# How the last sums of a mixture of experts are split between TensorE and VectorE, and how their rows are loaded and stored

## The chip, the cores and the metric

The kernel runs on one core of one Trainium2 chip. The metric is device time in microseconds, as the median of several runs. Beside these runs there is one profiled execution, from which the profile and the trace come. All times in views of the trace are microseconds from the start of its span.

## What is computed

The reference is a model of two layers, in fp32, on 8 sequences of 256 tokens with 256 features. Each layer is an attention-like block and a mixture of experts, and after each of the four blocks the result is added to the input and layer-normalised:

```python
x = L0_attn_x
x = _layernorm(x + _L0_attn_ref(x, ...), axis=-1)
x = _layernorm(x + _L0_ffn_ref(x, ...), axis=-1)
x = _layernorm(x + _L1_attn_ref(x, ...), axis=-1)
x = _layernorm(x + _L1_ffn_ref(x, ...), axis=-1)
```

Only the end of the last line matters here. `_L1_ffn_ref` routes every token to 4 of 16 experts, and adds a shared expert that sees all tokens:

```python
cw = _combine_weights(xt, gate_w)          # 4 nonzero weights per token
for e in range(E):
    a = _swiglu(xt @ expert_up_w[e].T)
    out = out + cw[:, e:e + 1] * (a @ expert_down_w[e].T)
out = out + _swiglu(xt @ shared_up_w.T) @ shared_down_w.T
```

So for each token four weighted rows of 256 numbers, the row of the shared expert and the token's own row are added, and the sum is normalised.

## The kernel before

The 2048 tokens are 16 tiles of 128 tokens (128 partitions), in 4 groups of 4 tiles (`GT = 4`, `NG = 4`). A group's residual rows stay in SBUF as `xg[g]`, 128 x 4 x 256. Attention, the first mixture, the state-space block and the second mixture follow each other.

In a mixture, tokens are first scattered to buckets by expert in HBM. Then tiles of 128 bucket rows run through the expert's three products; the weighted result of each row is scattered to HBM, to the tensor `m1ys`, where the four rows of a token lie side by side. The weights of all 16 experts lie meanwhile in one large SBUF tile, `big`.

What comes after the last expert tile is the tail, and the function `after1` writes it. For each of the 16 token tiles it has to:

- load the tile's results, 128 tokens x 4 rows x 256, 512 KB, from `m1ys` into a tile `m1gy` (`results`, L694, issued on SyncE's queue);
- add the four rows (`summed`): VectorE adds rows 0 and 1 to rows 2 and 3 (L751, a 128x512 add in place, "the halving add"), then TensorE multiplies each of the two halves with the identity matrix and adds them in PSUM (L756);
- add the PSUM sum to the residual row on VectorE (L759);
- normalise it (`normed`): statistics on VectorE (L720, L722), the inverse root on GpSimd (L731, L732, L734), a small product on VectorE (L733), scale and shift on ScalarE (L735);
- store the 128 KB of the finished tile from SyncE's queue (L1549).

The shared expert of the last group (tiles 12 to 15) is computed in the tail as well, with `Experts.shared`. It works on two halves of the group and three blocks of features: gate and up products (L543), a SiLU on ScalarE (L552) and a gate product on VectorE (L553), for each of six steps; and for each of the four tiles the down product (L563), into the PSUM bank to which L756 then adds the expert rows. The three steps of the first half come first; the others are interleaved with the sums of the other tiles by a list that is written out by hand, `order`: 0, 1, 12, 2, 3, 13, 4, 5, 6, 7, 14, 8, 9, 15, 10, 11. PSUM sums take turns in three banks.

Two pools of four buffers each hold the loaded results (`rowpool`, `lastrows`). Seven loads are issued ahead; each further load is issued after the code of one more tile, so on SyncE's queue loads and stores alternate:

```python
for n, i in enumerate(order):
    if i >= last:
        ...
        next(steps)
    else:
        finish(i)
    load(n + AHEAD)
```

The framework puts the instructions in order by its own priorities, engine by engine, and adds the waits. Each engine works through its list in that order. Each transfer of SyncE and ScalarE is given one of eight completion counters, in the order in which the framework places them, and waits until the transfer that had this counter before has landed.

Of the kernel before, what the change touches and what calls it, by code (L numbers as in the profile page):

```python
# [12 lines left out]
F32 = mybir.dt.float32  # L13
# [6 lines left out]
P = 128  # L20
DM = 256
KC = DM // P
NB, SEQ = 8, 256
GT = 4
# [9 lines left out]
E1, F1, TOP1, SH1 = 16, 176, 4, 352  # L34
# [53 lines left out]
M1 = Moe("m1", E1, F1, TOP1, 2, SH1, 5)  # L88
# [10 lines left out]
def kernel(  # L99
# [16 lines left out]
    nc = tc.nc  # L116
# [12 lines left out]
    def bank(tag, name):  # L129
        return psum.tile([P, 512], F32, name=name, tag=tag, bufs=BANKS[tag])  # L130

    x_rows = x_in.rearrange("b s d -> (b s) d")
    out_rows = out.rearrange("b s d -> (b s) d")
# [5 lines left out]
    xg = []  # L139
# [48 lines left out]
    for m in (M0, M1):  # L188
        d = disp[m.name] = {}
        new = lambda shape, name, dt=F32: const.tile(  # L190
            shape, dt, name=f"{m.name}{name}", tag=f"{m.name}{name}"
# [86 lines left out]
    def after_all(ins, first, done):  # L278

        if first is None:  # L280
            for w in done:
                tc.add_manual_dep(ins.ins, w.ins.name, SYNC, reason="reads what was written")
            return ins
        tc.add_manual_dep(ins.ins, first.ins.name, NOSYNC, reason="behind the first")
        return first
# [401 lines left out]
            with tc.If(count > m.usual - m.sure):  # L687
                run(m.usual, m.tiles)

    def results(m, g, t, pool=None):  # L690

        d, i = disp[m.name], g * GT + t
        gy = (pool or rowpool).tile([P, m.top, DM], F32, name=f"{m.name}gy{g}_{t}", tag="r")
        ins = nc.sync.dma_start(  # L694
            gy,
            d["ys"][i * P * m.top : (i + 1) * P * m.top, :].rearrange(
                "(p k) d -> p k d", k=m.top
            ),
        )
        d["first"] = after_all(ins, d["first"], d["results"])  # L700
        return gy
# [14 lines left out]
    def normed(g, t, by_steps=False):  # L716

        x = xg[g][:, t, :]
        st = small.tile([P, 6], F32, name="st", tag="st")
        nc.vector.bn_stats(st, x)  # L720
        mv = small.tile([P, 2], F32, name="mv", tag="mv")
        nc.vector.bn_aggr(mv, st)  # L722
        rstd = small.tile([P, 1], F32, name="rstd", tag="rstd")
        off = small.tile([P, 1], F32, name="off", tag="lnoff")
        if by_steps:
            var = small.tile([P, 1], F32, name="var", tag="rstd")
            nc.vector.tensor_scalar_add(var, mv[:, 1:2], LN_EPS)
            root_by_steps(rstd, var)
            nc.vector.scalar_tensor_tensor(off, mv[:, 0:1], -1.0, rstd, ALU.mult, ALU.mult)
        else:  # L730
            nc.gpsimd.tensor_scalar_add(rstd, mv[:, 1:2], LN_EPS)  # L731
            nc.gpsimd.tensor_tensor(rstd, rstd, root[:, :1], ALU.pow)  # L732
            nc.vector.tensor_scalar_mul(off, mv[:, 0:1], -1.0)  # L733
            nc.gpsimd.tensor_tensor(off, off, rstd, ALU.mult)  # L734
        nc.scalar.activation(x, x, AF.Identity, bias=off, scale=rstd)  # L735
# [8 lines left out]
            nc.vector.tensor_add(x, x, gy[:, k, :])  # L744
        normed(g, t)

    def summed(m, g, t, gy, y=None):

        half = m.top // 2
        x = xg[g][:, t, :]  # L750
        nc.vector.tensor_add(gy[:, :half, :], gy[:, :half, :], gy[:, half:, :])  # L751
        fresh = y is None
        if fresh:
            y = bank("a", f"{m.name}sum{g}_{t}")[:, :DM]
        for k in range(half):
            nc.tensor.matmul(  # L756
                y, lhsT=ident, rhs=gy[:, k, :], start=(fresh and k == 0), stop=(k == half - 1)
            )
        nc.vector.tensor_add(x, x, y)  # L759
        normed(g, t)  # L760
# [90 lines left out]
    rowpool = ctx.enter_context(tc.tile_pool(name="rows", bufs=4))  # L851
# [6 lines left out]
    big = bigpool.tile([P, SLOTS * SLOT], F32, name="big", tag="big")  # L858
# [246 lines left out]
    def after0(ex):  # L1105
        mixer_weights()
        for t in range(3):
            first[t] = results(M0, 0, t)
# [20 lines left out]
    with ExitStack() as st:  # L1129
# [14 lines left out]
        order, free = [], {}  # L1144
# [358 lines left out]
        def all_combined(g):  # L1503
            for t in range(GT):
                for i in (t, t + 1):
                    if i < GT and (g, i) not in waits:
                        waits[g, i] = results(M0, g, i)
                yield
                (summed if g < 2 else combined)(M0, g, t, waits.pop((g, t)))
                yield  # L1510
            ready.add(("combined", g))
# [17 lines left out]
    lastrows = ctx.enter_context(tc.tile_pool(name="lastrows", bufs=4, reuse_waits="tile"))  # L1529
# [4 lines left out]
    def after1(ex):  # L1534

        last = (NG - 1) * GT
        order = [0, 1, last, 2, 3, last + 1, 4, 5, 6, 7, last + 2, 8, 9, last + 3, 10, 11]
        pools = (rowpool, lastrows)
        AHEAD = 7
        rows = {}  # L1540

        def load(n):
            if n < len(order):
                rows[order[n]] = results(M1, *divmod(order[n], GT), pools[n % 2])

        def finish(i, y=None):
            g, t = divmod(i, GT)
            summed(M1, g, t, rows.pop(i), y)
            nc.sync.dma_start(out_rows[i * P : (i + 1) * P, :], xg[g][:, t, :])  # L1549

        for n in range(AHEAD):
            load(n)
        steps = ex.shared(NG - 1, wsh1, lambda t, y: finish(last + t, y))
        for _ in range(len(M1.shblocks)):
            next(steps)
        for n, i in enumerate(order):
            if i >= last:
                if i == last + 2:
                    next(steps)
                next(steps)  # L1560
            else:
                finish(i)
            load(n + AHEAD)

    mixture(M1, wsh1, (1, 2), (), after1)


# [91 lines left out]
```

## Time and profile before

| | us |
|---|---|
| median of 3 runs | 1518.86 (1517.16 to 1519.47) |
| the profiled execution | 1588.88 |
| its span | 1587.2 |
| the tail in it: from the first TensorE work after the last expert tile | 1542.66 to 1587.2 |
| last TensorE instruction of the tail ends | 1581.10 |
| last instruction of the normalisation (ScalarE) ends | 1584.22 |

| engine | busy in the span | instructions |
|---|---|---|
| TensorE | 1440.3 us (91%) | 6482 |
| VectorE | 814.7 us (51%) | 2962 |
| ScalarE | 576.9 us (36%) | 1498 |
| GpSimd | 426.5 us (27%) | 600 |

The profile comes from one execution with the hardware profiler on, which took 70 us longer than the median run. "PE" is TensorE's products, "PEld" its weight loads, "DVE" VectorE, "ACT" ScalarE, "POOL" GpSimd, "SPq" the issue of transfers on SyncE. L751 is line 751 of the kernel. The chain of waits follows the work that ended last back from the last instruction, at each step to what released it. A row of the timeline has its start, its length, the engine, the line, the operation with output and inputs, and in brackets how long the engine had been idle before it and what ended that. The mean granted clock of TensorE in the span is 0.955 of full speed. In the tail there are 16 loads of 512 KB and 16 stores of 128 KB.

### The profile page before, as it was taken

Reading aid. Unit: us, or ns where it says so; the run is one execution under the profiler, and the core shown is the slowest. Engines: PE = TensorE matmul, PEld = TensorE weight load, DVE = VectorE, ACT = ScalarE, POOL = GpSimd, SP = SyncE. Lnnn points to the kernel's source line nnn. Section 1 sums busy time; section 2 is a strip of 40 time slices with the busy share of each in tenths; the row PEclk is TensorE's granted clock in tenths of the full one; section 3 lists DMA queues with packets and bytes.
Section 4 is the critical chain, followed back from the end, with each engine's and each line's share of the span. In section 5 each row is a group of like instructions: output and inputs, shape, how many; then the busy total and the mean of one; then the engine's idle time right before and its main releaser. Section 6 shows DMA issues by size and latency. Waiting matters only on the chain. (4 is left out here: it accounts for less than half of the span.)

```text
span 1587.2 us, 21590 instructions
## 1 busy us (share of the span) xinstructions
PE 1440.3 (91%) x6482; PEld 1020.1 (64%) x6482; DVE 814.7 (51%) x2962; ACT 576.9 (36%) x1498; POOL 426.5 (27%) x600
## 2 busy tenths in 40 slices
PE   8999999999999999997898885898979768999997
PEld 5666665666566666675677773555656557677765
DVE  3444564455544554454354544676666454444436
ACT  3333433334233423351243432556646222233322
POOL 1000005000410031104635554021151442333334
PEclk9999999999999999997999998899989789999999
DMA  9999999800100020162444445310010631233327
GB/s 362 413 413 413 413 409 391 263 1 1 58 24 1 1 90 21 71 210 74 129 142 147 140 146 183 105 66 1 1 54 3 256 124 44 79 106 96 96 81 258
DMA packets 79973, 233.50 MB, mean 147 GB/s; under 512 B 11323, under 2 KB 44378, under 8 KB 78448
## 3 DMA queue, kind: packets, MB, share of 16 engines
q1 hardware_dynamic: 63088, 189.89, 33.7%
q0 software_dynamic: 16768, 42.19, 7.4%
q8 instruction: 56, 0.92, 0.3%
q14 instruction: 61, 0.50, 0.1%
HBM read 80.29 MB, written 155.40 MB: 149 GB/s over the span
## 5 line engine op out<-in xcount | busy, mean ns | idle before, releaser
L933 PE MATMUL qkp<-xT,big 128*128 128x512 f32 x512 | 243.0, 597 | 2.1 <-issue 2.1
L968 ACT ACTIVATE pr<-neg,least 128x128 f32<-128x128 f32 (+1 forms) x256 | 114.4, 449 | 281.8 <-DVE least L963 271.1
L671 POOL DMA_INDIRECT m0ys<-m0ys,m0xl x114 | 112.5, 987 | 99.6 <-ACT m0ys L670 37.3
L933 PEld LDWEIGHTS qkp<-xT,big 128*128 128x128 f32 x512 | 91.1, 191 | 72.5 <-issue 70.4
L941 DVE COPY qk<-qkp 128x512 f32<-128x512 f32 x64 | 44.1, 690 | 178.6 <-PE qkp L933 165.5
L371 POOL DMA_INDIRECT m0xs<-m0xe,m0rows x96 | 92.8, 966 | 154.6 <-DVE pT L984 109.4
L917 PE MATMUL vp<-big,xT 128*128 128x512 f32 x256 | 118.0, 599 | 4.3 <-DVE x L1004 4.3
L999 PE MATMUL op<-big,z 128*128 128x256 f32 x512 | 120.5, 382 | 0.0
L963 DVE CUSTOM_DVE_ANT_0 neg<-sc,cmask 128x128 f32<-128x128 f32 (+1 forms) x256 | 81.3, 354 | 63.9 <-PE sc L953 60.9
L671 POOL DMA_INDIRECT m1ys<-m1ys,m1xl x74 | 72.8, 984 | 115.5 <-ACT m1ys L670 104.3
L999 PEld LDWEIGHTS op<-big,z 128*128 128x128 f32 x512 | 92.6, 190 | 14.9 <-ACT z L1021 4.8
L259 POOL TENSOR_TENSOR rstd<-rstd,numbers 128x1 f32<-128x1 f32 x16 | 8.7, 551 | 305.9 <-DVE rstd L258 305.9
L986 PE MATMUL zp<-pT,big 128*128 128x256 f32 x256 | 77.9, 386 | 2.6 <-issue 2.0
L917 PEld LDWEIGHTS vp<-big,xT 128*128 128x128 f32 x256 | 47.1, 192 | 49.2 <-issue 42.2
L953 PE MATMUL sc<-qk,qk 128*128 128x256 f32 x256 | 77.9, 387 | 0.0
L974 DVE TENSOR_SCALAR pr<-pr,total 128x128 f32<-128x128 f32 (+1 forms) x256 | 70.2, 319 | 3.4
L984 DVE COPY pT<-pt 128x384 f32<-128x384 f32 x128 | 66.9, 549 | 5.9 <-issue 2.2
L986 PEld LDWEIGHTS zp<-pT,big 128*128 128x128 f32 x256 | 48.1, 192 | 33.8 <-issue 14.1
L980 PEld LDWEIGHTS pt<-ident,pr 128*128 128x128 f32 x384 | 47.6, 142 | 33.0 <-issue 30.4
L371 POOL DMA_INDIRECT m1xs<-m1xe,m1rows x64 | 62.1, 970 | 18.7 <-issue 17.0
L949 PEld LDWEIGHTS sc<-qk,qk 128*128 128x128 f32 x256 | 44.2, 193 | 29.6 <-issue 21.1
L980 PE MATMUL pt<-ident,pr 128*128 128x128 f32 x384 | 58.1, 274 | 0.0
(2808 smaller groups left out, 3032.7 us busy)
## 6 DMA issues: line engine op xcount, KB each, us to landing
m0xs<-blank SPq DMA_DIRECT2D x9, 7740.0 KB
m1xs<-blank SPq DMA_DIRECT2D x4, 7740.0 KB
m0xl<-m0xs SPq DMA_DIRECT2D x114, 129.0 KB
m0gy<-m0ys SPq DMA_DIRECT2D x16, 768.0 KB
m1xl<-m1xs SPq DMA_DIRECT2D x74, 129.0 KB
m1gy<-m1ys SPq DMA_DIRECT2D x16, 512.0 KB
big<-in_w_moe SPq DMA_DIRECT2D x1, 5472.0 KB
big<-in_w_heads SPq DMA_DIRECT2D x12, 384.0 KB
```

The costliest lines, as they stand in the source:

```text
L371: ins = nc.gpsimd.indirect_dma_start(out=d["xs"], out_offset=bass.IndirectOffsetOnAxis(ap=rows[:, k, t : t + 1], axis=0), in_=xe[:, k, :], ...
L671: ins = nc.gpsimd.indirect_dma_start(out=d["ys"], out_offset=bass.IndirectOffsetOnAxis(ap=row[:, DM : DM + 1].bitcast(I32), axis=0), in_=y ...
L917: nc.tensor.matmul(ps, lhsT=xT[:, k, t * P : (t + 1) * P], rhs=w_vq[q][:, k, :], start=(k == 0), stop=(k == KC - 1),)
L933: nc.tensor.matmul(ps, lhsT=w_qk[h][:, at : at + P], rhs=xT[:, k, :], start=(k == 0), stop=(k == KC - 1),)
L953: nc.tensor.matmul(sc[:, P:], lhsT=qT[:, c0 + P : c0 + SEQ], rhs=kT[:, c0 : c0 + SEQ], start=True, stop=True,)
L963: nc.vector.tensor_tensor_reduce(out=neg[:, cols], in0=sc[:, cols], in1=cmask[:, cols], scale=-SCALE, scalar=3.0e38, op0=ALU.add, op1=ALU.min,
L968: nc.scalar.activation(pr[:, cols], neg[:, cols], AF.Exp, bias=least[:, i : i + 1], scale=-1.0, accum_out=total[:, i : i + 1],)
L974: nc.vector.tensor_scalar_mul(pr[:, cols], pr[:, cols], total[:, i : i + 1])
L980: nc.tensor.transpose(pt[:, i * P : (i + 1) * P], pr[:, i * P : (i + 1) * P], ident)
L984: pace[0] = nc.vector.tensor_copy(pT, pt)
L986: nc.tensor.matmul(zps[:, b * SEQ : (b + 1) * SEQ], lhsT=vs[2 * b][:, cols], rhs=pT[:, : 2 * P], start=True, stop=False,)
L999: nc.tensor.matmul(ps[:, :DM], lhsT=zs[i][:, t * P : (t + 1) * P], rhs=w_o[q * QH + i], start=(i == 0), stop=(i == QH - 1),)
```

## The change

Four things change, all in the tail:

- For tiles with an odd number the halving add is left out, and TensorE adds all four rows with four products instead of two. Tiles with an even number are summed as before.
- The loaded results no longer take turns in two pools. Each of the 16 tiles has its own place in `big`, whose expert weights are no longer needed by then.
- All 16 loads are written ahead of the rest of the tail, instead of seven ahead and one after each tile.
- The finished tiles are stored from ScalarE's queue, not from SyncE's.

```diff
-    def results(m, g, t, pool=None):
+    def results(m, g, t, gy=None):
         d, i = disp[m.name], g * GT + t
-        gy = (pool or rowpool).tile([P, m.top, DM], F32, name=f"{m.name}gy{g}_{t}", tag="r")
+        if gy is None:
+            gy = rowpool.tile([P, m.top, DM], F32, name=f"{m.name}gy{g}_{t}", tag="r")
...
-    def summed(m, g, t, gy, y=None):
-        half = m.top // 2
+    def summed(m, g, t, gy, y=None, halved=True):
+        half = m.top // 2 if halved else m.top
         x = xg[g][:, t, :]
-        nc.vector.tensor_add(gy[:, :half, :], gy[:, :half, :], gy[:, half:, :])
+        if halved:
+            nc.vector.tensor_add(gy[:, :half, :], gy[:, :half, :], gy[:, half:, :])
...
-        pools = (rowpool, lastrows)
-        AHEAD = 7
         rows = {}
-        def load(n):
-            if n < len(order):
-                rows[order[n]] = results(M1, *divmod(order[n], GT), pools[n % 2])
+        for n, i in enumerate(order):
+            gy = big[:, n * TOP1 * DM : (n + 1) * TOP1 * DM]
+            rows[i] = results(M1, *divmod(i, GT), gy.rearrange("p (k d) -> p k d", d=DM))
         def finish(i, y=None):
             g, t = divmod(i, GT)
-            summed(M1, g, t, rows.pop(i), y)
-            nc.sync.dma_start(out_rows[i * P : (i + 1) * P, :], xg[g][:, t, :])
-        for n in range(AHEAD):
-            load(n)
+            summed(M1, g, t, rows.pop(i), y, halved=i % 2 == 0)
+            nc.scalar.dma_start(out_rows[i * P : (i + 1) * P, :], xg[g][:, t, :])
...
-        for n, i in enumerate(order):
+        for i in order:
...
-            load(n + AHEAD)
```

In the changed kernel's scheduled order, counted over SyncE's loads, load 8 waits for load 2, load 9 for load 3, load 10 for load 4, load 11 for the first store and load 12 for the second; loads 13 to 15 wait for loads 8 to 10, and load 16 for load 11. ScalarE's list has each store directly or nearly directly behind the normalisation that it waits for.

## The prediction

> **What bounds the kernel now.** The instructions ahead of the tail stand in the same order on every engine in both programs, so only the tail can move: the stretch from the last expert tile (first TensorE work of the tail at 1542.66 us) to the end of the span at 1587.2. I read the chain of waits first, for what ended last there; then the table of busy time by windows, cut where the chain changes character; then VectorE's and SyncE's own timelines.
>
> The chain, cut to the stretches that matter (start, duration, what):
>
> ```profile
> 1557.91 1.73 PE m1s_1gu L543 x8
> ...
> 1561.80 0.50 PE m1sum L756 x3
> 1562.31 6.17 DMA m1gy<-m1ys
> ...
> 1577.31 1.15 PE m1sum L756 x4
> 1578.45 0.02 issue
> 1578.47 0.42 DVE x L759
> 1578.89 0.61 DVE m1gy L751
> 1579.51 0.04 issue
> 1579.55 1.55 PE m1sum L756 x4
> ...
> 1583.62 0.60 ACT x L735
> ```
>
> Three regimes are seen. Until 1562.3 the chain is TensorE alone. Then one load of results takes 6.17 us from issue to use. From 1577 on the halving add on VectorE (L751), the sum on TensorE (L756) and the residual add on VectorE (L759) take turns, 2.24 us a tile (1579.55 - 1577.31), each waiting for the other. The windows say the same (length, then busy time of TensorE, its weight loads, VectorE, ScalarE, GpSimd; granted clock, DMA share, GB/s):
>
> ```profile
> 1542.66:1549.80 7.14, 7.08 (x24) 5.45 (x24) 1.10 (x3) 0.79 (x3) 0.98 (x1) 0.77 0.53 173
> 1549.80:1566.12 16.32, 16.02 (x72) 13.29 (x72) 13.96 (x47) 4.62 (x9) 8.15 (x22) 1.00 0.82 282
> 1566.12:1581.10 14.98, 10.59 (x40) 7.11 (x40) 11.00 (x34) 5.07 (x9) 9.57 (x23) 0.97 0.76 287
> 1581.10:1587.20 6.10, 0.00 (x0) 0.00 (x0) 1.18 (x4) 1.20 (x2) 1.22 (x5) 0.50 0.18 62
> ```
>
> TensorE is full until 1566 and holds 40 passes in the 15 us after that. Busy time flatters it, so I count passes. The chain counts eight passes for the four fp32 products of a shared block (two each) and gives them 1.73 us, 0.216 a pass. 24 + 72 + 40 = 136 passes are 29.4 us; the first eight ran at half clock (3.63 instead of 1.73 us), which makes 31.3. From 1542.66 to the last pass's end at 1581.10 are 38.4 us. **TensorE has 7.1 us of gaps in the tail**, nearly all after 1566. That is all there is to win there. Last, the rows that show where the late loads come from:
>
> ```profile
> 1561.13 0.37 SPq L694 DMA_DIRECT2D m1gy<-m1ys  x1
> 1561.87 0.34 SPq L1549 DMA_DIRECT2D out<-x  x1
> 1562.31 2.55 SPq L694 DMA_DIRECT2D m1gy<-m1ys  x1
> 1564.95 0.38 SPq L1549 DMA_DIRECT2D out<-x  x1
> ```
>
> Loads and stores alternate on SyncE's queue, so a load is issued only when an earlier tile is finished; the third row holds the queue for 2.55 us because its buffer is still being read.
>
> **The change part by part.** *More sums on TensorE.* Eight of 16 tiles get four products instead of two: 8 x 2 x 2 = 32 passes more, 32 x 0.216 = **6.9 us, all on the engine that is already full in the first half of the tail.** With no gap at all TensorE would need 168 x 0.216 + 1.9 = 38.2 us and end at 1580.9, only 0.2 before today's 1581.10. This is a floor: whatever loads and VectorE do, the end cannot come more than 0.2 us earlier. Half clock at the end of today's tail (the last sum took 1.55 us, the one before it 1.15) is one of the gaps and is counted in the 7.1.
>
> *Fewer halving adds on VectorE.* Eight of L751 at 0.684 us, 5.5 us less. Until 1566 VectorE's 13.96 us lie beside a fuller TensorE and are worth nothing; in the alternating stretch they are the gaps. They are already spent in the floor, so nothing more is credited.
>
> *Loads.* The seven at the head become 16 with buffers of their own in the expert weights' space, no longer interleaved with stores. They are not all in flight at once, though: each transfer takes one of eight completion counters and waits until the earlier transfer on its counter has landed. In the scheduled order loads 8, 9 and 10 wait for loads 2, 3 and 4, load 11 for the **first store**, load 12 for the second, and 13 to 16 stand behind them on SyncE. Load 2 landed at 1550.40 (VectorE's second halving add starts there), the next 1.27 us apart (512 KB at 415 GB/s), so loads 8 to 10 are issued by 1553 and keep the DMA engines busy. Load 11 depends on T, the landing of the first store. Its rows are ready at 1555.4, as now. The trace has no store issued by ScalarE, so I bound T. In the last store of the trace ScalarE ends at 1584.22 and the span at 1587.2: at most 3.0 us from ready to landed, T = 1558.4. If the store's data had to queue behind ten loads (seven moved by 1555.7, three more 3.8 us, then its own landing), T = 1561. Here a rule weighs in: the Trainium skill, "DMA: Bandwidth & Descriptors", section "Queues, rings and completion order", says that SyncE and ScalarE own separate rings on the same 16 DMA engines, which alternate between rings packet by packet. By it the store passes the waiting loads, T = 1558; by the trace alone, with one hardware queue in it, 1561. Its section "Issuing engines are not separate DMA queues" speaks against the change: another issuing engine saves only sequencer time. SyncE's 0.34 us per store is off the chain of waits but for the queueing, so I credit nothing for it.
>
> From T, load 11 lands about 4.0 us later (the first load: issued 1545.11, used 1549.12) and each further one 1.27 us later, four stores of 0.36 us mixed in: load 11 at 1562 to 1565, load 12 at 1563.5 to 1566.5, load 15 at 1568.5 to 1571.5. Who waits? VectorE's order puts load 11's halving add ahead of the residual adds of tiles whose sum buffers TensorE needs at about 1566.4; load 12's follows; load 15's stands ahead of the third shared block's gate product, which TensorE needs at about 1572. All three arrive in time or just in time. Cost taken: 0; upper end in the first rival.
>
> *Stores on ScalarE.* 16 issues. Lower bound nothing, if ScalarE's queue only passes them on; upper 0.44, the longest store issue on SyncE. I take 0.34, the median row. Below zero is excluded: the last store follows ScalarE's normalisation by 0.03 us today. ScalarE has 5.07 us of work in the third window, so 16 x 0.34 fits, with one exception. Each store waits for the normalisation ahead of it and holds everything behind it on ScalarE. The SiLU of the third block, needed by the shared expert's product for tile 14, stands behind two stores and one normalisation: 0.34 + 0.34 + 0.60 = 1.3 us late against TensorE's 1.3 us of other passes that hide it (SiLU 0.38 and gate product 0.41 come on top). That leaves a stall of about **0.9 us**; 0.2 with free issues, 1.1 with 0.44.
>
> *The sum.* TensorE: 1542.66 + 38.2 = 1580.9; starts that today's chain already shows as "issue" around the first sums 0.2; drain of the last pass 0.2; the SiLU's stall 0.9: last pass ends at 1582.2. The end chain is that of today (residual add, statistics, GpSimd's root, normalisation: 1581.10 to 1584.22, 3.1 us; the last tile has no halving add to delay it), then 3.0 to the end of the span. 1582.2 + 3.1 + 3.0 = **1588.3, that is 1.1 us later than 1587.2**. The profiled execution took 1588.88 us, 1.7 beyond its span, so it would take about 1590.1. The runs without the profiler have a median of 1518.86, 70 us less; nothing of that difference is in what this change touches, and I carry the microseconds over, with 0.1 for a tail that is a little tighter without the profiler: 1518.86 + 1.2 = 1520.1.
>
> **The rivals.**
>
> *Late loads hold VectorE (slower).* Place: VectorE's in-order queue, at the halving adds for loads 11, 12 and 15. Point from which it decides: T after about 1561, or less than some 380 GB/s. For it: load 10 of today took 5.8 us from issue (1561.13) to use (1566.90), and the second window moved only 282 GB/s with loads and stores mixed. Against it: that was a shallow queue, and with several loads queued the same mix moves 390 to 420 GB/s (1567 to 1576). Price: with T = 1561 and 282 GB/s, five loads and four stores (3.15 MB) take 11.2 us instead of 7.6, load 15 lands near 1574.4, 2.4 us after its need, and load 12 costs another 1.2. 1520.1 + 3.6 = 1523.7.
>
> *ScalarE's issues are dear (slower, less).* If an issue holds ScalarE for 0.7 us or more (both queues asking for descriptors at once near 1561), the SiLU's stall grows to some 1.6 us and the last normalisations queue behind stores by another 1: +1.7, 1521.8.
>
> *Gaps are larger in ordinary runs (faster).* If the 7.1 us of gaps are 11 or more without the profiler, removing them beats the 6.9 us of passes by over 3: 1515.5. The profile gives no reason for it; the floor speaks against it.
>
> *It does not load all at once* is not a separate case: six of 16 loads wait for stores, and the forecast already has it so.
>
> **How the numbers follow.** 0.2% is 3.0 us, about what a measurement of this kernel can tell from no change. The forecast has 0.57, late loads 0.28, dear issues 0.10, larger gaps 0.05. Within 0.2%: all of the forecast and half of the dear issues, 0.62; slower by more: late loads and the other half, 0.33; faster 0.05. Range: downward the floor (-0.2) and the scatter of the runs (1517.16 to 1519.47, 1.2 to each side), 1517.5; upward the late loads with a little margin, 1524.0.
>
> **What would show it.** Right: TensorE's gaps between 1550 and its last pass shrink from 7 to under 2 us with 168 passes in the tail, the chain of waits is nearly all TensorE, the last sum runs at full clock. Wrong: waits on DMA in front of the halving adds after 1562 (late loads); ScalarE's third SiLU starting over 2 us after its sums are done (dear issues); a tail whose TensorE ends before 1580.9, which would break the pass count itself.

## The result and the profile after

The changed kernel takes 1521.37 us (median of 22 runs, 1517.74 to 1527.06) against 1517.16 us before (median of 22 runs, 1512.10 to 1521.71). The ratio is 1.0026, with a 95% interval of 1.0015 to 1.0037: **3.9 us slower, between 2.3 and 5.6**. The prediction had 1.2 us slower. So the sign was right, and about 2.7 us are missing.

The kernel before takes 1517 us in these runs but 1588.88 in its profile and 1583 to 1590 beside the experiments, for a reason that is not shown and is not the profiler (the changed kernel's profiled execution took 1517.74), so only tails and ratios within one set of runs are compared.

All that lies ahead of the tail is the same work in the same order. The tail, from its first TensorE work to the end of the span, is 47.66 us (1468.34 to 1516.0) against 44.54: 3.1 us longer. TensorE's part of it, to the end of the last pass, is 41.57 against 38.44 us. The end chain (from there to the end of the last normalisation) is 3.15 against 3.12 and the rest 2.94 against 2.98. **All of the loss is in TensorE's part.** To compare times in the two traces, 74.32 us are added to those of the changed kernel (1542.66 - 1468.34).

The busy time of the changed kernel's tail by windows (start and end; length; busy time of TensorE, its weight loads, VectorE, ScalarE and GpSimd, with numbers of instructions; granted clock, DMA share, GB/s):

```profile
1468.34:1475.48 7.14, 7.06 (x24) 5.42 (x24) 1.16 (x3) 0.82 (x3) 0.98 (x1) 0.77 0.50 175
1475.48:1491.80 16.32, 16.27 (x75) 14.35 (x76) 9.75 (x29) 3.99 (x8) 4.91 (x15) 1.00 0.90 337
1491.80:1509.91 18.11, 15.60 (x70) 12.53 (x68) 11.70 (x44) 5.07 (x9) 9.21 (x27) 1.00 0.49 187
1509.91:1516.00 6.09, 0.00 (x0) 0.00 (x0) 1.19 (x4) 1.80 (x3) 2.06 (x7) 0.72 0.19 65
```

The first two windows are as predicted: TensorE is full, with more passes than before. The third isn't: 2.5 us of it are empty. (24 + 75 + 70 counts one pass twice that lies across a border; there are 168.) The chain of waits of the changed kernel (start, duration, what) says what TensorE waits for there. In this kernel L753 is the halving add, L758 the sum on TensorE, L761 the residual add, L736 the last step of the normalisation and L695 a load:

```profile
1480.38 7.35 DMA out<-x
1487.74 3.55 DMA big<-m1ys
...
1491.32 0.69 DVE big L753
...
1498.67 0.61 ACT x L736
...
1499.30 0.34 ACTq L1549
...
1499.69 0.39 ACT m1s_2s L552
...
1500.10 0.43 DVE m1s_2h L553
...
1500.57 0.70 PE m1s_2y L563 x2
```

The chain is not nearly all TensorE. Four rows belong beside it: what SyncE waited for in the tail (in total, times, longest), and rows of the timelines of VectorE and TensorE:

```profile
SPq L695 <- DMA out<-x: 8.9, 1, 8.9
1491.32 0.69 DVE L753 TENSOR_TENSOR big<-big 128x512 f32<-128x512 f32 x1 [2.42 <-DMA big<-m1ys]
1495.09 1.89 PE L543 MATMUL m1s_2gu<-m1xT,m1ws 128*96 128x256 f32 x8
1500.57 0.70 PE L563 MATMUL m1s_2y<-m1ws,m1s_2h 96*128 96x256 f32 x2 [2.30 <-DVE m1s_2h L553]
```

Read the chain downwards. The first store needs 7.35 us to land. Only then is the 11th load issued, since it takes over the store's completion counter: SyncE had been ready for it 8.9 us earlier. It lands 3.55 us later. VectorE has stood at that load's halving add for 2.42 us (its work before ended at 1488.90). This is the add of tile 14, whose sum TensorE starts only at 1501.1. But VectorE works in order, so residual adds and statistics of other tiles come late behind it. Behind these come GpSimd's roots, one after another (nearly all of the chain from 1495.71 to 1498.65), and then a normalisation on ScalarE (1498.67). Behind that normalisation and its store stands the third block's SiLU, though the gate and up products that it reads had been done since 1496.98, 2.7 us earlier. TensorE waits 2.30 us for what hangs on it.

Why does the store take so long? The DMA queues' packets in the changed kernel, in two stretches: from the store's issue to 1483.7, and then to 1485.5 (packets, MB, share of the 16 engines; q1 is SyncE's queue, q10 ScalarE's):

```profile
q1 hardware_dynamic: 359, 1.33, 102.1%
...
q1 hardware_dynamic: 164, 0.59, 81.0%
q10 hardware_dynamic: 114, 0.11, 17.6%
```

For 3.3 us after its issue not one packet of the store moves, though from 1482.05 on two stores are waiting on a queue of their own; only the loads' packets move. Ten loads have been issued by then, and some 2.0 MB of them, nearly four loads, are still to move. Then both queues share the engines. The store has landed at 1487.73, and a store that finds no load in flight, only another store, lands after 1.70 us (issued 1499.30, landed 1501.0). Meanwhile the loads run dry (the last number is GB/s):

```profile
1476.00:1486.00 10.00, 10.00 (x48) 8.78 (x48) 7.48 (x23) 2.18 (x4) 3.73 (x11) 1.00 1.02 401
1486.00:1489.00 3.00, 3.00 (x16) 2.63 (x15) 1.35 (x4) 1.47 (x3) 1.18 (x4) 1.00 0.47 131
```

### The profile page after: what moved, and what is told of

The parts are those of the page before. It is cut to its first block, busy times and chain, and to the rows that moved or that the text cites. A ratio compares the mean times of both kernels' runs of the same rounds, so it can differ in the third digit from the quotient of the medians.

```text
span 1516.0 us, 21612 instructions
## 1 busy us (share of the span) xinstructions
PE 1420.3 (94%) x6514; PEld 1014.4 (67%) x6514; DVE 812.5 (54%) x2954; ACT 578.8 (38%) x1498; POOL 424.4 (28%) x600
## 4 chain that ended last, share of the span: by engine, by line
PE 67%; issue 11%; POOL 9%; DMA 6%; DVE 5%; ACT 2%; POOLq 0%; SPq 0%; DVEq 0%; ACTq 0%
PE qkp L935 15%; PE vp L919 7%; PE op L1001 6%; POOL m1ys L671 4%; PE zp L988 4%; PE sc L955 4%; PE pt L982 3%; DMA m0ys<-m0ys,m0xl 2%; PE sc L951 2%; PE zp L992 2%; PE cv L1186 2%; PE out L1486 2%; POOL m1xs L371 2%; PE sg L1297 2%; POOL m0ys L671 1%
## 5 line engine op out<-in xcount | busy, mean ns | idle before, releaser
L919 PEld LDWEIGHTS vp<-big,xT 128*128 128x128 f32 x256 | 47.2, 193 | 49.4 <-issue 42.4
L988 PEld LDWEIGHTS zp<-pT,big 128*128 128x128 f32 x256 | 47.7, 190 | 30.4 <-issue 12.0
L736 ACT ACTIVATE x<-x,off,rstd 128x256 f32<-128x256 f32 x48 | 28.7, 598 | 81.3 <-POOL off L735 74.1
```

Source lines behind the costliest of these rows:

```text
L919: nc.tensor.matmul(ps, lhsT=xT[:, k, t * P : (t + 1) * P], rhs=w_vq[q][:, k, :], start=(k == 0), stop=(k == KC - 1),)
L988: nc.tensor.matmul(zps[:, b * SEQ : (b + 1) * SEQ], lhsT=vs[2 * b][:, cols], rhs=pT[:, : 2 * P], start=True, stop=False,)
```

## The experiments

Each ratio is to runs of the kernel before beside it and has an interval of about 0.2% to each side, 3 us. So by run times alone e1, e2 and e10 are like before, and their intervals also overlap those of the changed kernel. Smaller steps rest on the trace of one profiled execution of each kernel. The one kernel that was profiled twice, the changed one, has tails of 47.7 and 49.4 us, so a difference of one or two microseconds between tails counts only where the waits in the traces account for it. "Loads" says when the loads are issued, "odd" whether odd tiles are added by TensorE alone.

| kernel | loads | odd | stores | TensorE's part, us | end chain, us | tail, us | ratio to before (95%) |
|---|---|---|---|---|---|---|---|
| before | as they come | no | SyncE | 38.4 | 3.1 | 44.5 | 1 |
| changed | at once | yes | ScalarE | 41.6 | 3.1 | 47.7 | 1.0026 (1.0015 to 1.0037) |
| e9, changed again | at once | yes | ScalarE | 43.3 | 3.1 | 49.4 | 1.0032 (1.0015 to 1.0049) |
| e1 | at once | yes | SyncE | 38.7 | 3.1 | 44.8 | 0.9997 (0.9974 to 1.0020) |
| e2 | at once | yes | 5 SyncE, 11 ScalarE | 39.3 | 3.1 | 45.3 | 1.0006 (0.9983 to 1.0029) |
| e10, SiLU earlier | at once | yes | ScalarE | 38.9 | 3.1 | 45.1 | 1.0001 (0.9980 to 1.0023) |
| e4 | as they come | yes | SyncE | 41.1 | 3.1 | 47.2 | 1.0020 (1.0002 to 1.0037) |
| e3 | at once | no | ScalarE | 34.2 | 4.5 | 41.6 | 0.9975 (0.9959 to 0.9991) |
| e6 | at once | no | SyncE | 34.2 | 4.5 | 41.6 | 0.9982 (0.9964 to 1.0000) |
| e7 | as they come | no | ScalarE | 36.6 | 4.8 | 44.4 | 0.9992 (0.9972 to 1.0012) |
| e5, all 16 tiles | at once | all | SyncE | 47.7 | 3.1 | 53.8 | 1.0057 (1.0034 to 1.0080) |
| e8, first and last tile | at once | two | SyncE | 34.7 | 3.1 | 40.7 | 0.9982 (0.9966 to 0.9999) |
| e11, e8 with SiLU earlier | at once | two | SyncE | 33.1 | 3.1 | 39.1 | 0.9963 (0.9948 to 0.9977) |

Three theories of the loss: **A**, the late 11th load, by way of VectorE, the normalisations and the SiLU; **B**, the 32 passes on a full TensorE; **C**, ScalarE's issues ahead of the SiLU.

**e1: stores back on SyncE's queue.**

```diff
-            nc.scalar.dma_start(out_rows[i * P : (i + 1) * P, :], xg[g][:, t, :])
+            nc.sync.dma_start(out_rows[i * P : (i + 1) * P, :], xg[g][:, t, :])
```

> The changed kernel with its 16 stores back on SyncE's queue, behind all loads; TensorE's, VectorE's and GpSimd's order are those of the changed kernel. No load waits for a store any more. Theory A (late loads: the 11th load waits for the first store, which lands behind ten queued loads; VectorE waits for it, the normalisations come late, the third SiLU stands behind them on ScalarE and TensorE stalls 2.3 us): load 11 is issued about 10 us earlier, no halving add waits more than 0.5 us on a DMA after the first, TensorE's gap ahead of the third block of tile 14's product shrinks from 2.3 to under 1 us, and the time falls by 2 to 3 us against the changed kernel, to 1518.5 to 1519.5. Theory B (the 32 passes are the whole cost, TensorE is full): as the changed kernel, 1521, ratio 1.0026. Theory C (ScalarE's store issues ahead of the SiLU are the cost): also 2 to 2.5 us less, but with VectorE's wait for load 11 unimportant.

The tail is 44.8 us, 2.9 less than the changed kernel's. VectorE waits for a load once, for the first. The chain of waits is TensorE alone from the first pass to the last; its stretch around the old gap:

```profile
1567.21 0.86 PE m1s_2y L563 x4
1568.07 0.43 PE m1sum L758 x2
1568.50 0.65 PE m1s_2y L563 x2
```

The third product of tile 14 follows with no wait. TensorE's part is 38.68 us, where the prediction had a floor of 38.2 and 0.4 for starts and drain. A and C both allow this; B, as the whole cost, does not.

**e2: the stores of the first five tiles on SyncE, the others on ScalarE**, so that no load waits for a store but the SiLU still has four stores ahead of it.

```diff
-            nc.scalar.dma_start(out_rows[i * P : (i + 1) * P, :], xg[g][:, t, :])
+            store = nc.sync if order.index(i) < 5 else nc.scalar
+            store.dma_start(out_rows[i * P : (i + 1) * P, :], xg[g][:, t, :])
```

> As the changed kernel, but the stores of the first five tiles in the order go to SyncE's queue behind the loads, the other eleven stay on ScalarE. No load waits for a store; the third SiLU still stands behind four stores on ScalarE. Theory A: as with all stores on SyncE (within 0.7 us of it), 1518.5 to 1519.5; the issues themselves cost TensorE under 1 us. Theory C: as the changed kernel, 1521, with the SiLU over 2 us after its sums and TensorE's gap of 2 us in place. Theory B: 1521 too, but without a gap.

The tail is 45.3, 0.6 more than e1's 44.8. TensorE's timeline (start, length, line and shapes; in brackets the idle time before and what ended it):

```profile
1570.16 0.59 PE L758 MATMUL m1sum<-big,ident 128*128 128x256 f32 x2
1571.23 0.70 PE L563 MATMUL m1s_2y<-m1ws,m1s_2h 96*128 96x256 f32 x2 [0.47 <-DVE m1s_2h L553]
```

The stall behind the SiLU is 0.47 us instead of 2.30. So ScalarE's issues are a minor part, and C falls as the main cause. What e2 takes away, the counter that load and store share and the first five issues on ScalarE, makes up 2.3 of the 2.9 us (47.66 - 45.34).

**e10: the third block's step written earlier**, so that its SiLU is no longer behind the late normalisations; loads, stores and passes as in the changed kernel.

```diff
         for i in order:
+            if i == 5:
+                next(steps)
             if i >= last:
-                if i == last + 2:
-                    next(steps)
                 next(steps)
```

> The changed kernel with one step moved: the third shared block of the second half (gate and up products, SiLU, gate product) is written ahead of tile 5 instead of ahead of tile 14, so that its SiLU is not behind the normalisations that come late. Loads, stores, passes and counters are the same. If the last link of theory A holds (late normalisations ahead of that SiLU turn the late load into TensorE's gap): the 2.3 us gap is gone, VectorE still waits over 2 us for load 11, the tail is 1.5 to 2.5 us shorter than the changed kernel's. If TensorE is held by the sum buffers as well, which VectorE frees late, the gap comes back in another place and the tail shortens by under 1 us.

The chain of waits has the same two late transfers at its head, and then:

```profile
1555.78 7.11 DMA out<-x
1562.91 4.00 DMA big<-m1ys
...
1571.34 0.42 DVE m1s_2h L553
1571.76 0.34 DVE x L761
...
1572.14 1.56 PE m1s_2y L563 x6
```

VectorE still stands 2.63 us at the 11th load, but TensorE's stall in front of tile 14's product is 0.23 us, and the tail is 45.1, 2.6 less than in the first profile of the changed kernel. So the last link of A is shown too: here the late load costs TensorE almost nothing by itself; it costs 2.3 us because the SiLU is queued behind what it delays.

**e9: the changed kernel again**, beside the other experiments.

> The changed kernel unchanged, on the chip on which the other experiments ran. If the tail is what differs and the late loads are a fixed part of it: a tail of 47 to 48.3 us (47.7 in the first profile), first store landing 7 to 8 us after its issue, one halving add waiting over 2 us for load 11, TensorE's gap of 2 us ahead of the third block's product for tile 14; ratio to before 1.001 to 1.004. If these waits were an accident of one execution, the tail is 45 to 46 us.

The wait for the store (7.05 us on the chain) and TensorE's gap come back. The tail is 49.4, longer than expected, and the ratio 1.0032. The added 1.7 us lie right behind the gap (its row of the timeline, then windows as above):

```profile
1575.69 0.84 PE L563 MATMUL m1s_2y<-m1ws,m1s_2h 96*128 96x256 f32 x2 [2.30 <-DVE m1s_2h L553]
1572.50:1575.69 3.19, 0.89 (x6) 0.44 (x4) 1.22 (x4) 1.71 (x4) 2.11 (x5) 1.00 0.42 143
1575.69:1578.23 2.54, 2.54 (x7) 2.07 (x8) 0.00 (x0) 0.00 (x0) 0.00 (x0) 0.58 0.15 53
```

After the same gap the granted clock is 0.58 for 2.5 us here, and in the first profile it stays at 1.00. (The first passes of the tail ran at full clock here, which the first load then took back: TensorE stood 1.51 us at the first sum.) So the gap costs 2.3 us or some 4, and the changed kernel's tail is 3.1 or 4.9 us longer than before's; the runs' 3.9 lies between. How often each happens two profiles do not tell.

**e4: only the odd tiles' passes, in the kernel before.** `summed` gets the flag `halved`, and `after1` passes `halved=i % 2 == 0`; pools, loads and stores stay.

> The kernel before (two pools, seven loads ahead, stores on SyncE) with only the extra passes: odd tiles are added by TensorE alone. Theory A: the passes fill gaps that are there anyway: 0 to 1.5 us slower than before (ratio 1.000 to 1.001). Theory B: 3 to 5 us slower, ratio 1.002 to 1.003, with TensorE full until the last sums.

2.7 us more in the tail, ratio 1.0020. Theory A had 0 to 1.5 us and so falls in the form in which it was stated: **the passes are not free in the loads' old rhythm**. This kernel's waits show a gap of its own, again in front of tile 14's third product, behind that SiLU (in total, times, longest):

```profile
PE m1s_2y L563 <- DVE m1s_2h L553: 2.4, 1, 2.4
```

**e3: the changed kernel with every tile halved** (`halved=i % 2 == 0` removed), and **e6**, the same with the stores on SyncE: before with all loads at once and nothing else.

> As the changed kernel, but every tile keeps its halving add (no extra passes on TensorE). Loads at once and stores from ScalarE stay. Theory A: TensorE has 6.9 us less to do but is held by the late loads; loads after the 11th still wait for stores; the time falls by 1 to 3 us, to 1518.5 to 1520. Theory B: the passes were the cost: 1521.4 less 5 to 6.9, VectorE being the next bound: 1514.5 to 1516.5, faster than the kernel before.

> The kernel before with one part of the change alone: all 16 loads at once in places of their own; halving adds in all tiles and stores on SyncE. Theory A (late loads cost, extra passes only fill): late loads are gone without the passes; VectorE is the next bound; the tail is 40.5 to 42 us against 44.5 before, 2.5 to 4 us faster, ratio 0.9975 to 0.9985, and a little shorter than with the stores on ScalarE (41.65). Rival: with loads at once but all halving adds VectorE and TensorE alternate at the end as before, the gaps stay, tail 44 to 45.

Both tails are 41.6 us, 2.9 shorter than before. e3's is 6 us shorter than the changed kernel's, as theory B expected (5 to 6.9; A 1 to 3), and e6 is what its text expected of A. e6's windows:

```profile
1543.00:1558.00 15.00, 15.00 (x71) 13.12 (x70) 13.74 (x42) 4.04 (x8) 8.24 (x18) 1.00 1.03 411
1558.00:1570.19 12.19, 10.58 (x48) 8.22 (x46) 9.82 (x36) 3.88 (x7) 7.43 (x21) 1.00 0.53 194
```

The transfers run at 411 GB/s in the first stretch, and TensorE has 1.6 us of gaps in the second. All of it (1.61 us) is in the same place again, in front of tile 14's third product, here without a late load. The chain of waits reaches that SiLU through GpSimd's part of the normalisations (1558.74 to 1562.91). Loading at once is worth 2.9 us of the tail alone (ratio 0.9982, with 1.0000 at the edge of its interval); the passes spend it: with them the tail is 44.8 (e1), 3.2 more. So the passes cost 3.2 us with all loads at once and 2.7 in the old rhythm (e4), under half of the 6.9 us that TensorE needs for them. B is a part of the loss and not the whole; A is the other.

ScalarE's stores, which cost 2.9 us where odd tiles go to TensorE, show no cost in e3. The load is late there too: SyncE waits 5.6 us for the first store and issues load 11 at 1559.75, 7.3 us after that store. But VectorE, with every halving add to do, comes to this load's only at 1563.43 and does not wait for it. That the two tails are equal is not exact, though: e6 lost 0.9 us more than e3 to the lower clock in its first 16 passes.

**e5: no halving add at all, stores on SyncE** (`halved=False`), twice the extra passes.

> As the kernel with all loads at once and stores on SyncE, but no tile has a halving add: TensorE adds all four rows of all 16 tiles, 32 passes more. If TensorE is the bound there and a pass costs 0.216 us: TensorE's part of the tail grows from 38.7 to 45.6 us and the tail from 44.8 to 51.7, 7.2 us longer than before's 44.5, ratio 1.0045. If instead VectorE or the transfers still hold the tail, it grows by under 4 us.

TensorE's part is 47.7, 9.0 more than in e1, where 6.9 was expected. The chain accounts for the rest: the second block's eight passes take 2.99 us instead of 1.73 (the granted clock is 0.55 over the first 6.9 us, against 0.77 over 7.1 in the changed kernel), and 0.9 us are a stall behind the third SiLU. The pass count holds.

**e7: the kernel before with stores from ScalarE's queue.**

> The kernel before with only its stores moved to ScalarE's queue. The first store then finds about two loads in flight instead of five. If a store waits its turn behind the loads already queued, it lands about 4 us after its issue here (against 7.3 in the changed kernel and 1.7 with nothing in flight); if the rings took turns packet by packet, under 2.5 us in both. The tail: loads no longer stand behind stores that wait on SyncE, 1 to 3 us shorter than before's 44.5; if ScalarE's issues are dear, longer.

A miss in both points. The tail is 44.4, not 1 to 3 us shorter. TensorE ran at full clock from the start here, stood 1.7 us at the first halving add, and then had a clock of 0.78 for 4 us. And a load still stands behind a store: SyncE waits 5.4 us for one, and its next load is issued at 1554.11, 7.2 us after the first store. The trace gives no landing of that store. Its first packets move about 2.6 us after its issue (in the changed kernel 3.3, in e9 at least as much), with only the loads' packets until then. So it waits here too, and a landing in under 2.5 us is excluded; how the wait grows with the queue is not settled by this.

**e8: two tiles only**, the first of the order and the last (`halved=i not in (0, 11)`), stores on SyncE, and **e11**, the same with the edit of e10.

> All loads at once, stores on SyncE, and only two tiles added by TensorE alone: the first in the order (its rows are waited for, with VectorE idle) and the last (nothing is left behind it to fill TensorE). 8 passes are 1.7 us more for TensorE, which has slack in the halved kernel; the halving add drops out of the first sum and of the end chain. Expected: tail 40 to 41.5 us, 0 to 1 us shorter than with all halved; 3 to 4.5 us faster than before, ratio 0.9972 to 0.9982. Theory B (any extra pass costs): 1.7 us longer than with all halved.

> The fastest version so far (all loads at once, stores on SyncE, only the first and the last tile of the order added by TensorE alone) with the third shared block written ahead of tile 5 as well. TensorE's gap of 1.3 us ahead of tile 14's third product goes; VectorE is then the bound for longer. Expected: tail 39.5 to 40.7 us (40.7 without the step moved), ratio to before 0.997 to 0.998.

e8 has a tail of 40.7, with a gap of 1.34 us in front of tile 14's third product. In e11 that gap is gone and the tail is 39.1, a little under what was expected and 5.5 us shorter than before, with a ratio of 0.9963 (0.9948 to 0.9977). **e11 beats both kernels.** Its windows:

```profile
1558.20:1574.00 15.80, 15.80 (x75) 13.68 (x74) 13.66 (x43) 4.30 (x9) 7.59 (x17) 1.00 1.03 410
1574.00:1584.17 10.17, 10.17 (x48) 8.58 (x46) 9.40 (x36) 4.80 (x8) 8.61 (x24) 1.00 0.61 222
```

TensorE is busy to the last pass and VectorE nearly is (23.1 of 26.0 us): the work is balanced, with 144 passes instead of 168.

## Why the prediction came out as it did

- *The passes: 6.9 us, and a floor of 38.2 us for TensorE.* Right. e1 reaches 38.68 with 0.4 for starts and drain. That nothing could be won was rightly read from it, and so the sign had a reason. In e2, where ScalarE issues stores but no load is late, the tail is 0.8 us longer than before, near the 1.1 of the forecast; that so small a step is there at all, neither its run times nor one profile can tell for sure. What the text did not say is that the loads alone would have won 2.9 us (e6), which the passes spend.
- *Loads: "All three arrive in time or just in time. Cost taken: 0".* **This is the step that failed**, in two places. First the landing of the first store, T: taken between 1558 and 1561, measured 1562.05 in the times of the trace of before (1487.73 + 74.32, the distance between the two tails' starts). The lower end rested on the Trainium skill's page "DMA: Bandwidth & Descriptors", section "Queues, rings and completion order", read as if single packets of the two rings alternated from the store's issue on. The trace shows no packet of the store for 3.3 us, so the measurement decides against that reading; the same section lets a packet hold up to 64 descriptors, and no run here shows where the border lies. The upper end, a store behind all ten loads, is nearer: the loads' packets end at about 1485.9 (1560.2, where 1559.5 was taken), and the store lands 1.9 us later. Secondly the need: it was dated by the sum buffers, for which TensorE waited only 0.21 us. The way on which it cost was another: VectorE arrived at load 11's halving add at 1563.2 in the time of before, was held until 1565.6, and everything behind it in VectorE's order, the statistics above all, came late to ScalarE. The term was put at 0 and measured 2.3 us.
- *Stores: 0.34 us each, the third SiLU 0.9 us late for TensorE.* The size of an issue is right (338 ns, the median of all 16). The stall is too high when nothing else is late (0.47 in e2), and too low with the late load (2.30). The SiLU was seen to stand behind two stores and a normalisation; that this normalisation itself could be late was left out. The two risks were priced apart, and they are one chain.
- *The sum: last pass 39.5 us after the tail's start.* It is 41.57: e1's 38.68, the gap of 2.30, 0.21 at the sum buffers, and 0.4 that stay unassigned. End chain 3.1 (3.15) and rest 3.0 (2.94) are right. Counted as the prediction counts them, TensorE's gaps are 3.4 us (41.57 - 168 x 0.216 - 1.9): fewer than the 7.1 of before, but not under 2.
- *The rivals.* "Late loads hold VectorE", given 0.28, is what happened, by its own point of decision (T after about 1561), with 1523.7 as its time: 3.6 us for the late loads, where the runs show 2.3. Its price was worked out from a rate of 282 GB/s and the lateness of load 15; the rate did not fall like this while loads were queued (337 in the second window), and the cost came from load 11. "ScalarE's issues are dear" had the same visible sign, a third SiLU over 2 us after its sums, and was still wrong: e2 has the issues without the lateness. "Gaps are larger in ordinary runs" has nothing for it; the difference of 70 us that it leant on was not the profiler's.

## What to carry to other kernels

When a store moves to another engine's queue, look up whose completion counter it takes, and who takes it next: a store whose data is ready late can hold back a load that has nothing to do with it. When a transfer becomes late, follow it through every in-order queue behind the waiting instruction, to the one short step that another engine needs, instead of asking only when its own result is needed. And keep the parts of a change apart: here one of them alone gains 2.9 us of the tail, and two others spend that and more.

## What the hardware showed that was not expected

- A store of 128 KB, issued while some 2.0 MB of loads on another queue were still to move, landed after 7.35 us (7.05 in e9), against 1.70 with only another store in flight; its first packets moved after 3.3 us or more.
- After one and the same gap of TensorE, 2.30 us, the granted clock fell to 0.58 for 2.5 us in one profile (e9) and stayed at 1.00 in another of the same kernel.
- At the start of the tail, after 2.7 to 3.4 us without work, a clock of about a half costs 1.9 to 2.0 us of the first 16 passes in nine of the 13 profiles, 2.8 in e6 and 3.3 in e5. In e7 and e9, which had stood shortest (2.73 and 2.76 us), it costs 0.3 or less, but e11, with 2.79, is among the nine.
